# Window attention on one core: order and width of the score products on the tiles of TensorE

## The chip, the cores and the metric

The kernel runs on one core of a Trainium2 chip. The metric is the time of one execution on the device in microseconds. Before the change the median of three runs is 4113.76 us (4112.39 to 4114.41). A profile is one further execution, recorded instruction by instruction.

## The reference

The input x has 16 images of 56 x 56 positions with 384 channels, in fp32. Two layers follow each other.

```python
x = x + window_attention(group_norm(x, 32))
x = x + depthwise_3x3(group_norm(x, 32), sign(clip(w)))
```

The attention shifts the image by 3, cuts it into windows of 7 x 7 = 49 positions and works in each window with 12 heads of 32 channels:

```python
score = einsum('bhwqd,bhwkd->bhwqk', q, k) / sqrt(32) + rel[q, k]
# last row and last column of windows: -inf where q and k lie on different sides of the shift
attn = softmax(score)
out = einsum('bhwqk,bhwkd->bhwqd', attn, v) @ w_out.T + b_out
```

Everything is computed in fp32.

## The kernel before

An image is worked through in 8 strips of one row of windows (8 windows, 392 positions), each strip in two units of four windows. This gives 16 x 8 x 2 = 256 units. Channels lie on the 128 partitions in three blocks; a block holds four heads of 32 channels, so head i of a block lies on partitions 32i to 32i + 31.

For each strip TensorE makes queries and keys (`query_key`, L472, six blocks of 128 x 392), values (`value`, L485, three blocks) and the output projection (`project`, L655, three blocks), each with three accumulated matmuls. For each unit it makes the scores (`scores`, L526), the sums of the exponentials (`add_up`, L596) and the product with the values (`attend`, L616).

In a unit the four windows are two pairs: r is the pair, w the window of the pair. `scores` makes, for each block j, window w, pair r and head i, one product of 32 channels. Its weights (the stationary operand) are 64 columns of keys that begin with the 49 of the window, its moving operand the 49 queries. The result goes to partitions 64w to 64w + 63 of the PSUM bank i. A product thus uses 32 rows of the array, chosen by i, and 64 columns, chosen by w: one of eight tiles. With the loops in the order j, w, r, i, four products in a row go to four tiles, the next four (the other r) to the same four, and then w changes. The 15 rows behind the 49 keys receive products with keys of the next window, and nobody uses them.

`softmax` (L543, VectorE) reads all four banks, scales and adds a bias; `exponential` (L561, ScalarE) takes the exponential of all 128 rows in place and keeps a sum of each row, which after the last unit is only tested for being below 1e17. `add_up` writes into two of the four banks of the same scores tile (on all 128 partitions), where ScalarE (L634) and VectorE (L636) read it. The bias comes from `load_bias`, which fills a mask with zeros, loads its 2 x 49 valid rows from memory, and from `add_bias`. If the tests after the last unit fail, the program computes everything again with a softmax that subtracts the maximum (`fast` is False there, and keys and queries change places in `scores`).

The order of instructions is written out by hand (`manual_schedule`). `all_units` runs for each unit the heavy work in six steps, puts `scores` and `softmax` of the next unit behind the third or fourth of them, and fills in the light work (loading the next image, the convolution of the previous one) by due times. The steady order on TensorE over one strip is: sums and attention of the first unit, values and scores, queries and keys, sums and attention of the second unit, queries and keys, a third of the projection, scores, the rest of the projection, values. The convolution runs on VectorE (`tap`, L783), its input and the first image's come through the queues of POOL and SP. The scores tile has one buffer of four PSUM banks (`ps_s`); the other four banks go in turn to all other products (`ps`, `bank`).

Of the kernel before, what the change touches and what calls it, by code (L numbers as in the profile page):

```python
# [9 lines left out]
F32 = mybir.dt.float32  # L10
# [9 lines left out]
NEG = -1.0e30  # L20
# [14 lines left out]
def kernel(  # L35
# [12 lines left out]
    nc = tc.nc  # L48
    P = 128
    B, H, W, C = x.shape  # L50
    NH = rel_table.shape[1]
    D = C // NH
    NC = C // P
    HPC = P // D
    T = WIN * WIN
# [3 lines left out]
    UW = 4  # L59
    UPS = NW // UW  # L60
    NU = NS * UPS
    HT = 64
# [24 lines left out]
    small = ctx.enter_context(tc.tile_pool(name="small", bufs=2))  # L87
    ps_s = ctx.enter_context(tc.tile_pool(name="ps_s", bufs=1, space=bass.MemoryType.PSUM))
    ps = ctx.enter_context(tc.tile_pool(name="ps", bufs=4, space=bass.MemoryType.PSUM))

    def bank(name):
        return ps.tile([P, 512], F32, tag="mm", name=name)
# [18 lines left out]
    qk = const.tile([P, 2 * NC, ST + HT - T], F32, tag="qk", name="qk")  # L111
# [19 lines left out]
    def clear():  # L131
        for xl in xls:
            nc.gpsimd.memset(xl[:, NL - 1, :], 0.0)

        for t in spare:
            nc.gpsimd.memset(t[:, NL - 1, :], 0.0)

    def clear_more():
        nc.gpsimd.memset(power, -0.5)
        nc.gpsimd.memset(ones, 1.0)  # L140
        nc.gpsimd.memset(least, LEAST)
        nc.gpsimd.memset(seen, 0.0)
        for t in (qk[:, :, ST:], *hps, *accs):
            nc.gpsimd.memset(t, 0.0)
# [7 lines left out]
    def fetch_weights():  # L152

        rows = [w[r * P : (r + 1) * P, :] for w in (w_qkv, w_out) for r in range(w.shape[0] // P)]
        for n in range(0, len(rows), NC):
            wl = xpool.tile([P, NC, ST], F32, tag="x", name=f"wl_{n}")
            for k in range(NC):
                nc.scalar.dma_start(wl[:, k, :C], rows[n + k])
            staged.append(wl)

    def load_weights(n):

        for k in range(NC):
            pw = bank(f"pw_{n}_{k}")
            for c in range(NC):
                nc.tensor.transpose(pw[:, c * P : (c + 1) * P], staged[n][:, k, c * P : (c + 1) * P], ident)
            dst, r = (wq_t, NC * n + k) if n < NC else (wo_t, k)
            copy = nc.scalar.copy if k == 1 else nc.vector.tensor_copy
            copy(dst[:, :, r * P : (r + 1) * P], pw[:, : NC * P].rearrange("p (c q) -> p c q", c=NC))
# [20 lines left out]
    def load_bias(queue, first_q, last_q, fast):  # L190


        if not loaded_bias:
            rel = ypool.tile([P, NC, WIN, R], F32, tag="y", name="rel").rearrange("q c h w -> q (c h w)")[:, : T * NH]
            nc.gpsimd.memset(rel, 0.0)
            loaded_bias.append(rel)
        rel = loaded_bias[0]
        flat = rel.rearrange("q (a n) -> q a n", a=WIN)
        for q in range(first_q, last_q):
            qr, qc = divmod(q, WIN)  # L200
            first = qr * REL + qc if fast else (WIN - 1 - qr) * REL + (WIN - 1 - qc)
            row = rel_table[first : first + 1, :]
            src = bass.AP(
                tensor=row.tensor,
                offset=row.offset,
                ap=[[NH, 1], [REL * NH, WIN], [1, WIN * NH]],
            )
            queue.dma_start(flat[q : q + 1], src)
        if last_q < T:
            return  # L210
        queue.dma_start(flat[HT : HT + T], flat[0:T])
        mask = ypool.tile([P, NC, WIN, R], F32, tag="y", name="mask").rearrange("q c h w -> q (c h w)")[:, : 2 * T]
        mask = mask.rearrange("q (v k) -> q v k", v=2)
        nc.gpsimd.memset(mask, 0.0)
        for w in range(2):
            queue.dma_start(mask[w * HT : w * HT + T], wmask[0:T, :, 0:T])
        loaded_bias.append(mask)
# [151 lines left out]
    def fetch(s):  # L369
        b, r = divmod(s, NS)  # L370
        xl = staging(s)
        first = r * WIN + SHIFT
        for odd in range(2):
            t, end = 0, (WIN + 1 - odd) // 2
            while t < end:
                row = (first + odd + 2 * t) % H
                n = min(end - t, (H - row + 1) // 2)
                rows = x[b, row : row + 2 * n - 1 : 2].rearrange("t w c -> w t c")
                here = xl[odd * W : (odd + 1) * W, t : t + n, :]
                for lo, hi in ((SHIFT, SHIFT + 48), (SHIFT + 48, W), (W, R)):  # L380
                    nc.sync.dma_start(here[lo - SHIFT : hi - SHIFT], rows[lo % W : (hi - 1) % W + 1])
                t += n

    def load(s, c):
        b, r = divmod(s, NS)
        if (0, b) not in stats:
            stats[0, b] = small.tile([P, NC, NS, 6], F32, tag="st0", name=f"st0_{b}", bufs=1)
        if c == 0:
            xs[s] = xpool.tile([P, NC, ST], F32, tag="x", name=f"x_{s}")
        pt = bank(f"pl_{s}_{c}")  # L390
        for t in range(NL):

            n = min(LT, max(ST - t * LT, HT + 1))
            nc.tensor.transpose(
                pt[:, t * LT : t * LT + n], staging(s)[:n, t, c * P : (c + 1) * P], ident[:n, :n]
            )
        nc.scalar.copy(
            xs[s][:, c, :].rearrange("p (w r c) -> p r w c", r=WIN, c=WIN),
            pt[:, :ST].rearrange("p (r w c) -> p r w c", w=NW, c=WIN),
        )  # L400
        nc.vector.bn_stats(stats[0, b][:, c, r, :], xs[s][:, c, :])
# [111 lines left out]
    def scores(u, fast):  # L513


        s, n = divmod(u, UPS)
        pp = ps_s.tile([P, HPC, 512], F32, tag="s", name=f"ps_{u}")
        for j in range(NC):
            for w in range(2):
                for r in range(2):  # L520
                    for i in range(HPC):
                        part = slice(i * D, (i + 1) * D)
                        q0 = (n * UW + 2 * r + w) * T
                        row, col = (w, r) if fast else (r, w)
                        k0 = (2 * j + col) * T
                        nc.tensor.matmul(  # L526
                            pp[row * HT : (row + 1) * HT, i, k0 : k0 + T],
                            qk[part, NC * fast + j, q0 : q0 + HT],
                            qk[part, NC * (not fast) + j, q0 : q0 + T],
                            start=True,  # L530
                            stop=True,
                        )
        raw[u] = pp

    def softmax(u, fast):
# [482 lines left out]
    with tc.manual_schedule():  # L1018
        nc.scalar.preload_act_table_set("natural_log_exp_and_others")
        clear()  # L1020
        staged.append(None)
        for s in range(2 + len(spare)):
            fetch(s)
        staged.clear()
        fetch_weights()
        clear_more()
        load_bias(nc.gpsimd, 0, 38, True)
        for s in range(NS):
            for c in range(NC):
                load(s, c)  # L1030
            if s + 2 + len(spare) < NS:
                fetch(s + 2 + len(spare))
            if s % 2 and s > 1:
                load_weights(s // 2 - 1)
        norm_gather((0, 0), nc.sync)
        clear_again()
        for xl in xls:
            nc.gpsimd.memset(xl, 0.0)
        norm_scale((0, 0), nc.sync, nc.vector)
        load_bias(nc.gpsimd, 38, T, True)  # L1040
        load_weights(NC)
        load_depthwise()
        add_bias(True)
        normalize(0)
        all_units(True)


        worst = small.tile([P, 2], F32, tag="worst", name="worst")
        for n in range(2):
            nc.vector.tensor_scalar(reach[:, n], reach[:, n], MOST[n], None, ALU.is_lt)  # L1050
        nc.vector.tensor_reduce(worst[:, 0:1], reach.rearrange("p n u -> p (n u)"), AX.X, ALU.min)
        fine = small.tile([P, B + NC], F32, tag="fine", name="fine")
        nc.vector.tensor_scalar(fine, seen, 1.0e37, None, ALU.is_lt)
        nc.vector.tensor_reduce(worst[:, 1:2], fine, AX.X, ALU.min)
        pf = bank("pf")
        nc.tensor.matmul(pf[:, 0:2], ones, worst, start=True, stop=True)
        both = small.tile([P, 1], F32, tag="both_fine", name="both_fine")
        nc.vector.tensor_reduce(both, pf[:, 0:2], AX.X, ALU.add)
        nc.vector.tensor_scalar(again, both, -1.0, 2.0 * P, ALU.mult, ALU.add)
# [65 lines left out]
```

## Time and profile before

| | |
|---|---|
| median of the runs | 4113.76 us |
| profiled execution | 4109.91 us, span 4108.1 us |
| TensorE matmuls busy | 4017.7 us (98%) |
| TensorE weight loads busy | 2490.6 us |
| VectorE busy | 3496.3 us (85%) |
| ScalarE busy | 2236.7 us (54%) |
| GpSimd busy | 1873.2 us (46%) |
| scores, L526 | 24576 matmul passes and 24576 weight loads |

PE stands for matmuls, PEld for the weight loads, which overlap them; DVE is VectorE, ACT ScalarE, POOL GpSimd, SP the engine that only issues transfers. In a line of the groups, the part behind the names gives the size of the weights (rows * columns) and the shape of the moving operand, then the count, the busy time in us with the mean of one in ns, and the idle time of the engine ahead of them with what ended it. An fp32 product appears as two weight loads and two matmul passes. Busy time counts a moment once, however many passes overlap in it; the durations of single passes are modelled, their starts are not.

### The profile page before, as it was taken

What the parts mean: (1) busy time and instruction counts of PE and PEld (TensorE: products, weight loads), DVE (VectorE), ACT (ScalarE), POOL (GpSimd) and SP (SyncE); (2) the same over time, 40 slices, a digit from 0 to 9 for tenths busy, and PEclk for the clock granted to TensorE, in tenths of its full rate; (3) what the DMA queues carried; (4) which work ended last, traced back from release to release, by engine and by line L of the source; (5) the groups of instructions that cost most, each with busy time, mean ns of one, the idle gap of its engine ahead of it and who ended that gap; (6) DMA issues with size and microseconds to landing.
All of it is one profiled execution on the core that took longest, in us unless ns stands there. A gap on an engine that the chain in (4) does not pass through costs nothing.

```text
span 4108.1 us, 144986 instructions
## 1 busy us (share of the span) xinstructions
PE 4017.7 (98%) x63161; PEld 2490.6 (61%) x63161; DVE 3496.3 (85%) x3711; ACT 2236.7 (54%) x4654; POOL 1873.2 (46%) x3165
## 2 busy tenths in 40 slices
PE   5999999999999999999999999999999999999997
PEld 3666666666666666666666666666666666666656
DVE  4555989889898998989889898998989889898897
ACT  2545646555555655655555564655656555565552
POOL 5444535545453555545445452554545455452100
PEclk8999999999999999999999999999999999999998
DMA  4434556555655655556565655655556565554544
GB/s 94 78 61 89 111 101 126 106 107 103 118 114 110 117 110 108 111 98 127 107 114 104 112 115 105 117 117 100 114 101 122 105 123 109 102 123 77 108 101 110
DMA packets 1523990, 438.92 MB, mean 107 GB/s; under 512 B 1458970, under 2 KB 1473979, under 8 KB 1523346
## 3 DMA queue, kind: packets, MB, share of 16 engines
q1 hardware_dynamic: 1432680, 267.66, 38.1%
q0 software_dynamic: 87648, 159.12, 15.4%
q8 instruction: 499, 8.18, 0.8%
q10 hardware_dynamic: 3018, 2.78, 0.3%
q14 instruction: 145, 1.19, 0.1%
HBM read 169.63 MB, written 158.46 MB: 80 GB/s over the span
## 4 chain that ended last, share of the span: by engine, by line
PE 50%; issue 18%; POOL 13%; DVE 8%; DMA 7%; SPq 2%; ACT 1%; DVEq 0%; ACTq 0%; POOLq 0%
PE pq L472 21%; PE pv L485 10%; PE py L655 9%; POOL xl L419 8%; PE ps L526 4%; DVE o L783 4%; PE po L616 3%; DMA mvd<-mv 2%; PE ps L596 2%; POOL dev L268 2%; DMA xl<-in_x_dram 1%; DMA gt<-mvd 1%; SPq L508 1%; DMA mid<-y 1%; DVE e L543 1%
## 5 line engine op out<-in xcount | busy, mean ns | idle before, releaser
L472 PE MATMUL pq<-xn,wq_t 128*128 128x392 f32 x4608 | 1586.7, 497 | 0.1
L419 POOL DMA_DIRECT2D xl<-in_x_dram x1980 | 1332.9, 723 | 147.3 <-DVE xt L436 92.7
L783 DVE SCALAR_TENSOR_TENSOR o<-hp,dw_t,o 128x1568 f32<-128x1568 f32 x752 | 1378.8, 1834 | 5.4
L472 PEld LDWEIGHTS pq<-xn,wq_t 128*128 128x128 f32 x4608 | 846.2, 188 | 596.3 <-issue 1.5
L485 PE MATMUL pv<-xn,wq_t 128*128 128x392 f32 x2304 | 815.9, 497 | 8.1 <-DVE y L663 7.0
L655 PE MATMUL py<-ot,wo_t 128*128 128x392 f32 x2304 | 816.4, 499 | 3.0 <-DVE ot L644 3.0
L479 ACT COPY qk<-pq 128x392 f32<-128x392 f32 x768 | 369.4, 483 | 641.5 <-PE pq L472 640.3
L675 POOL COPY y<-y 128x63 f32<-128x63 f32 x128 | 53.3, 416 | 1320.8 <-DVE y L663 1320.8
L485 PEld LDWEIGHTS pv<-xn,wq_t 128*128 128x128 f32 x2304 | 424.2, 188 | 308.2 <-DVE y L663 8.7
L655 PEld LDWEIGHTS py<-ot,wo_t 128*128 128x128 f32 x2304 | 426.4, 190 | 300.1 <-DVE ot L644 10.5
L561 ACT ACTIVATE e<-e 128x1176 f32<-128x1176 f32 x256 | 303.2, 1184 | 439.0 <-DVE e L543 437.9
L636 DVE SCALAR_TENSOR_TENSOR ln<-ps,inv 128x588 f32<-128x588 f32 x256 | 196.1, 766 | 368.5 <-ACT inv L635 367.9
L492 ACT COPY vt<-pv 128x392 f32<-128x392 f32 x384 | 189.2, 493 | 411.9 <-PE pv L485 411.8
L526 PEld LDWEIGHTS ps<-qk 32*64 32x64 f32 x24576 | 307.2, 131 | 144.5 <-issue 108.3
L616 PEld LDWEIGHTS po<-e,v 49*32 49x32 f32 x24576 | 352.2, 105 | 55.5 <-issue 11.4
L543 DVE SCALAR_TENSOR_TENSOR e<-ps,bias 128x1176 f32<-128x1176 f32 x256 | 347.4, 1357 | 12.6 <-PE ps L526 12.2
L616 PE MATMUL po<-e,v 49*32 49x49 f32 x24576 | 345.5, 212 | 10.3 <-DMA v<-vq 9.6
L526 PE MATMUL ps<-qk 32*64 32x49 f32 x24576 | 339.3, 226 | 2.0 <-DVE ln L636 2.0
L448 ACT COPY x<-xt 128x196 f32<-128x196 f32 x720 | 225.6, 368 | 178.3 <-DVE xt L436 178.1
L496 DVE STREAM_TRANSPOSE vq<-vt 128x512 f32<-128x512 f32 x384 | 266.0, 694 | 9.9 <-ACT vt L492 6.5
L663 DVE TENSOR_TENSOR y<-py,x 128x392 f32<-128x392 f32 x384 | 213.6, 556 | 48.2 <-PE py L655 44.7
L461 ACT ACTIVATE xn<-x,coef 128x392 f32<-128x392 f32 x384 | 247.1, 711 | 13.2 <-DMA coef<-cod 13.2
(173 smaller groups left out, 3287.4 us busy)
## 6 DMA issues: line engine op xcount, KB each, us to landing
v<-vq SPq DMA_DIRECT2D x2048, 48.0 KB
xb<-mid SPq DMA_DIRECT2D x90, 855.5 KB
out_dram<-o SPq DMA_DIRECT2D x736, 98.0 KB
mid<-y POOLq DMA_DIRECT2D x112, 619.5 KB
xl<-in_x_dram POOLq DMA_DIRECT2D x1260, 52.5 KB
mid<-y POOLq DMA_DIRECT2D x15, 354.0 KB
xl<-in_x_dram POOLq DMA_DIRECT2D x180, 28.0 KB
mid<-y POOLq DMA_DIRECT2D x15, 265.5 KB
```

The source lines that it names most:

```text
L419: nc.gpsimd.dma_start(xz[i * D + lo : i * D + hi, c, k : k + n, :], flat[token : token + n * (hi - lo)].rearrange("(k t) c -> t k c", k=n) ...
L461: nc.scalar.activation(xn[:, c, :, :T], xs[s][:, c, :].rearrange("p (w t) -> p w t", t=T), AF.Identity, bias=coef[:, c, 1:2], scale=coef[: ...
L472: nc.tensor.matmul(pq[:, :ST].rearrange("p (w t) -> p w t", t=T), wq_t[:, c, m * P : (m + 1) * P], xn[:, c, :, :T], start=(c == 0), stop=( ...
L479: nc.scalar.copy(qk[:, m, :ST], pq[:, :ST])
L485: nc.tensor.matmul(pv[:, :ST].rearrange("p (w t) -> p w t", t=T), wq_t[:, c, 2 * C + m * P : 2 * C + (m + 1) * P], xn[:, c, :, :T], start= ...
L496: nc.vector.transpose(vq[:, :, :, m].rearrange("p h n d -> p n h d"), vt[:, m].rearrange("p (n w) (j b) -> p n (w j) b", w=2, b=D),)
L526: nc.tensor.matmul(pp[row * HT : (row + 1) * HT, i, k0 : k0 + T], qk[part, NC * fast + j, q0 : q0 + HT], qk[part, NC * (not fast) + j, q0 ...
L543: nc.vector.scalar_tensor_tensor(e, pp[:, :, : NC * 2 * T].rearrange("q i (n k) -> q i n k", k=T), QSCALE, bias[:, int(s % NS == NS - 1)]. ...
L561: nc.scalar.activation(flat, flat, AF.Exp, accum_out=reach[:, 0, u : u + 1])
L616: nc.tensor.matmul(po[w][i * D : (i + 1) * D, (2 * j + r) * T : (2 * j + r + 1) * T], vs[s][keys, n * 2 + r, h * D : (h + 1) * D], by_head ...
L655: nc.tensor.matmul(py[:, :ST], wo_t[:, c, m * P : (m + 1) * P], ots[s][:, c, :], start=(c == 0), stop=(c == NC - 1),)
L783: nc.vector.scalar_tensor_tensor(acc, by_half(hp[:, dy : dy + BR, dx : dx + W]), dw_t[:, c, t : t + 1], acc, ALU.mult, ALU.add)
```

## The change

In `scores` the loops over w, r and i become a loop over r and one over eight values k, which takes the heads 0 to 3 twice and alternates w: head i with w = 0, 1, 0, 1 in the first four and w = 1, 0, 1, 0 in the second four. Eight products in a row go to eight tiles. The weights are the 49 keys alone, and the output is 49 rows. The rows between the windows are therefore no longer written by `scores`: they hold zeros from a clearing at the start, or sums that `add_up` wrote there. For them the mask is filled with -1e30 where it was 0, so that their exponentials are zero. The scores tile is made once, ahead of the loops, in place of once per unit. In the second computation (`fast` False) the weights keep 64 columns and the mask keeps zeros.

```diff
+    score_banks = ps_s.tile([P, HPC, 512], F32, tag="s", name="score_banks")
...
-        nc.gpsimd.memset(mask, 0.0)
+        nc.gpsimd.memset(mask, NEG if fast else 0.0)
...
-        pp = ps_s.tile([P, HPC, 512], F32, tag="s", name=f"ps_{u}")
+        pp = score_banks
+        rows = T if fast else HT
         for j in range(NC):
-            for w in range(2):
-                for r in range(2):
-                    for i in range(HPC):
-                        part = slice(i * D, (i + 1) * D)
-                        q0 = (n * UW + 2 * r + w) * T
-                        row, col = (w, r) if fast else (r, w)
-                        k0 = (2 * j + col) * T
-                        nc.tensor.matmul(
-                            pp[row * HT : (row + 1) * HT, i, k0 : k0 + T],
-                            qk[part, NC * fast + j, q0 : q0 + HT],
-                            qk[part, NC * (not fast) + j, q0 : q0 + T],
-                            start=True,
-                            stop=True,
-                        )
+            for r in range(2):
+                for k in range(2 * HPC):
+                    i, w = k % HPC, (k + k // HPC) % 2
+                    part = slice(i * D, (i + 1) * D)
+                    q0 = (n * UW + 2 * r + w) * T
+                    row, col = (w, r) if fast else (r, w)
+                    k0 = (2 * j + col) * T
+                    nc.tensor.matmul(
+                        pp[row * HT : row * HT + rows, i, k0 : k0 + T],
+                        qk[part, NC * fast + j, q0 : q0 + rows],
+                        qk[part, NC * (not fast) + j, q0 : q0 + T],
+                        start=True,
+                        stop=True,
+                    )
...
         clear()
+        nc.vector.memset(score_banks, 0.0)
```

## The prediction

> **What bounds the kernel now.** I read the engines' shares of the span first, then the busy times of the steady middle.
>
> ```profile
> PE 4017.7 (98%) x63161; PEld 2490.6 (61%) x63161; DVE 3496.3 (85%) x3711; ACT 2236.7 (54%) x4654; POOL 1873.2 (46%) x3165
> 2000.00:3000.00 1000.00, 997.25 (x15955) 610.56 (x15951) 888.87 (x928) 568.70 (x1188) 500.31 (x836) 1.00 0.58 111
> ```
>
> In the second line the numbers after the length are PE, PEld, DVE, ACT and POOL. TensorE is never out of work: 997 of 1000 us, at full clock. DVE is next with 889. So the time is the sum of TensorE's batches, and a microsecond taken out of one comes off the span, until DVE is reached. Next the groups of instructions for the scores (L526), the attention product (L616) and the operation that reads the scores.
>
> ```profile
> L526 PEld LDWEIGHTS ps<-qk 32*64 32x64 f32 x24576 | 307.2, 131 | 144.5 <-issue 108.3
> L543 DVE SCALAR_TENSOR_TENSOR e<-ps,bias 128x1176 f32<-128x1176 f32 x256 | 347.4, 1357 | 12.6 <-PE ps L526 12.2
> L616 PE MATMUL po<-e,v 49*32 49x49 f32 x24576 | 345.5, 212 | 10.3 <-DMA v<-vq 9.6
> L526 PE MATMUL ps<-qk 32*64 32x49 f32 x24576 | 339.3, 226 | 2.0 <-DVE ln L636 2.0
> ```
>
> 24576 = 256 batches x 96: each of the 48 fp32 products of a batch is two weight loads and two matmul passes. A busy PE isn't a fast PE, since these overlap: the price of a batch is the distance from its first start to the start of the next batch. The timeline of PE over one strip gives it.
>
> ```profile
> 2030.37 1.14 PE L616 MATMUL po<-e,v 49*32 49x49 f32 x96
> 2031.45 4.22 PE L485 MATMUL pv<-xn,wq_t 128*128 128x392 f32 x12
> 2035.59 1.32 PE L526 MATMUL ps<-qk 32*64 32x49 f32 x96
> 2036.84 8.17 PE L472 MATMUL pq<-xn,wq_t 128*128 128x392 f32 x24
> ```
>
> Scores: 2036.84 - 2035.59 = 1.25 us. Attention, with as many passes of as many columns and eight tiles in rotation (two row groups by four column groups): 2031.45 - 2030.37 = 1.08 us. Read start by start from the trace, the scores take 1.246 us almost every time (127 of 127 where query_key follows, within 0.1 us; 96 of 127 within 0.02 us where project follows). The attention's best is 1.072 us, met on both of its places.
>
> Where do the scores lose? Busy times by stretch, of L526 alone, all from one beginning, so that each count tells how many passes (first count) and loads (second) have begun:
>
> ```profile
> 2005.20:2005.38 0.18, 0.10 (x9) 0.10 (x12) 1.00 0.00 0
> 2005.20:2005.58 0.38, 0.30 (x33) 0.30 (x34) 1.00 0.00 0
> 2005.20:2005.78 0.58, 0.50 (x43) 0.50 (x45) 1.00 0.00 0
> 2005.20:2005.98 0.78, 0.70 (x62) 0.70 (x66) 1.00 0.07 2
> 2005.20:2006.18 0.98, 0.90 (x83) 0.90 (x85) 1.00 0.10 3
> 2005.20:2006.38 1.18, 1.10 (x96) 1.10 (x96) 1.00 0.09 3
> ```
>
> and the same for an attention batch:
>
> ```profile
> 2030.30:2030.57 0.27, 0.20 (x19) 0.27 (x16) 1.00 0.48 66
> 2030.30:2030.77 0.47, 0.40 (x36) 0.47 (x36) 1.00 0.32 44
> 2030.30:2030.97 0.67, 0.60 (x60) 0.67 (x60) 1.00 0.23 31
> 2030.30:2031.17 0.87, 0.80 (x82) 0.87 (x81) 1.00 0.17 24
> ```
>
> Three parts in a scores batch. (1) By 2005.58, 0.30 us in, 34 loads (17 products) have begun: these were queued already. (2) A hole: the 35th load starts 0.344 us in. (3) The other 31 products take until about 1.10 us, 10 passes per 0.1 us (43 to 83 in 0.40 us), where the attention does 12 (36 to 60 in 0.20 us), that is 16.7 ns a product. Single starts show why. Loads of four neighbours are 16.7 ns apart (344, 361, 378, 394 ns), then a load for a tile used four products ago waits: 394 to 461, and 117 ns lie between two first loads of one tile. Where the loop changes w, the next four go to other tiles and there is no wait (511, 528, 544, 561 ns). So the loop's two values of r, which hit the same four tiles one after the other, cost about 50 ns once per eight products.
>
> **The Trainium skill.** "TensorEngine Tiling (Array Packing)", Key Properties, says different tiles run loads and matmuls in parallel, and 32x64 has eight. The trace agrees where w changes. "TensorE: Matmul & The Clock Gate", Part 3, says a load overlaps matmuls in flight only when the row group differs. Here the trace differs: the loads at 528 to 561 ns go to row groups whose matmuls on the other column tile had just begun (515 to 565 ns). The same page, LDWEIGHTS, prices a load at columns / 1.2 ns: 53 ns for 64, 41 for 49; the trace has 55 ns from a tile's first load to its second (344 to 399), and no 49-column load. "Runtime: NRT & Kernel Launch", Instruction fetch mechanics, says instructions come in 16 KiB blocks of 256, mostly hidden. The page shows 499 packets and 8.18 MB on the instruction queue, 16.4 KB each; whether it is hidden matters below.
>
> **The change part by part.**
> Order and width. Products on one tile are now eight apart: 8 x 16.7 = 133 ns, against the 117 ns a tile needs now and an estimated 117 - 2 x 12 = 93 with 49 columns. The wait goes. What is next is the issue of instructions, 16.7 ns a product. A batch then is: start of the 18th product 0.344 us (unchanged), 30 further products x 16.7 = 0.501, one load and one pass until the last pass begins, 41 + 41 ns = 0.08 (my estimate, 49 columns or rows at 1.2 per ns), and 0.145 us from the last pass to the next batch as now. Sum 1.07 us, against 1.246; the attention's clean 1.072 says the same. The hole is uncertain: if the queue refills because something finishes, the first product ends earlier (its load is shorter by 12 ns); if because the queue runs empty, eight tiles empty it at the 6.6 ns a pass with which the attention opens, 34 x 6.6 = 0.22, + 0.057 for the gap seen now = 0.28 us, another 0.06 less. Between both I take 1.056, a gain of 0.19 us; ends 0.174 and 0.25.
>
> Issue stalls. Now a late instruction is caught by the backlog: sequencer 16.7 ns a product, array 24.4 ((1.10 - 0.344) / 31). With the array waiting for the sequencer it isn't. The attention shows the price: of its 127 batches ahead of query_key the mean is 1.185 us, 0.113 over the best, with holes of 60 to 110 ns at changing places. Per product, 0.113 / 39 (nine are queued at its start), so 31 products could lose 0.09 us. Against that, the scores ahead of query_key show not one late batch now, those ahead of project 31 of 127. I take half, 0.045; ends 0 and 0.09.
>
> Net 0.19 - 0.045 = 0.145 us x 256 = 37 us. Ends: (0.174 - 0.09) x 256 = 22 and 0.25 x 256 = 64.
>
> One tile for all units in place of one per unit: in the built order of TensorE's instructions the waits stand where they stood: at the first product on DVE in half of the batches, at the 1st, 17th and 33rd on ACT in the others. Nothing. The clearing of the tile: one DVE operation, 2048 elements a row; by L543 (1176 in 1.357 us) an estimated 2.4 us, while DVE does nothing until 17.33 us. Uncovered it would cost those 2.4. The mask's fill has another value and the same size. DVE's and ACT's operations keep their shapes; the rows between windows hold old sums or zeros plus the mask, so their exponentials are zero. No DMA is added or moved. The matmuls behind the scores start earlier; in the steady middle DVE goes from 0.889 to 0.898 of the time (30.6 us a strip less 0.29), so it stays behind.
>
> Against the profiled execution, 4109.91 us (span 4108.1), this gives 4073; the median of the runs shown is 3.9 above it, and I take that as base: 4113.8 - 37 = 4077.
>
> **Rivals.**
> (A) As above, stalls partly seen: 25 to 50 us, 4064 to 4089.
> (B) The refill comes earlier and stalls stay hidden: 50 to 70 us, 4044 to 4064. For it: the hole starts just after the last queued load (287 ns). Against: the attention stalls.
> (C) Stalls in full, or DVE's taps (1.8 us each) make TensorE wait for banks more often (now 7.0 us at L485): 8 to 25 us, 4089 to 4105.
> (D) The change doesn't do what it says: something else than the tile sets 24.4 ns a product, for instance a limit per row group of 93 ns for four: 31 / 4 x 93 = 0.72 against 0.756 us, 0.04 us, or nothing: 4104 to 4114. Against: the eight loads in one run.
> (E) Slower: taking turns between two column tiles of one row group makes each load wait for the pass in flight there, as the skill's sentence would have it, with both passes of both products in line: 4 x 41 = 164 ns for four products, 41 each; 31 x (41 - 24.4) = 0.51 us, 132 us: 4245. It decides from 24.4 ns a product on. Against: the same eight loads; for: the trace shows such a turn only once per eight products, and no load of 49 columns.
>
> **How the numbers follow.** A 0.60, B 0.13, C 0.14, D 0.06, E and other ways to lose 0.07. A measurement of this kernel can tell about 0.2%, 8.2 us. Faster: A, B, C and a bit of D, 0.88; same 0.05; slower 0.07. The range takes in A and most of B and C: 4055 to 4100.
>
> **What would show it.** Scores batches of about 1.06 us with a tail of later ones up to 1.2; loads of 49 columns, and eight loads 16.7 ns apart in one run; still 12 passes per 0.1 us after the hole. TensorE as busy as before and DVE near 0.90. Wrong, if passes stay at 10 per 0.1 us (D), fall below it (E), or if batches after the scores grow longer (C).

## The result and the profile after

The changed kernel takes 4081.35 us (median of 4 runs, 4078.99 to 4082.26) beside 4113.34 us before; the ratio is 0.9925, with a 95% interval of 0.9912 to 0.9937. That is 32 us less, where 37 were forecast. A later series of the same kernel gave 4083.65 beside 4113.10 us (ratio 0.9929, 0.9915 to 0.9942), 29 us less. The profiled execution has a span of 4079.4 us, 28.7 below that of before.

First the engines' shares and the steady middle of the kernel after, in the order PE, PEld, DVE, ACT, POOL:

```profile
PE 3981.1 (98%) x63161; PEld 2447.1 (60%) x63161; DVE 3495.8 (86%) x3712; ACT 2231.7 (55%) x4654; POOL 1870.2 (46%) x3165
2000.00:3000.00 1000.00, 994.95 (x16087) 604.45 (x16087) 896.86 (x937) 566.29 (x1189) 495.10 (x835) 1.00 0.60 113
```

DVE went from 889 to 897 us in the 1000. TensorE is still nearly always busy, but its idle time in this stretch grew from 2.75 to 5.05 us. The groups (lines have moved: L529 was L526, L619 was L616, L546 was L543):

```profile
L619 PE MATMUL po<-e,v 49*32 49x49 f32 x24576 | 347.1, 212 | 13.4 <-DMA v<-vq 11.9 <-issue 0.2
L546 DVE SCALAR_TENSOR_TENSOR e<-score_banks,bias 128x1176 f32<-128x1176 f32 x256 | 347.2, 1356 | 10.7 <-PE score_banks L529 10.7
L529 PE MATMUL score_banks<-qk 32*49 32x49 f32 x24576 | 298.2, 218 | 2.6 <-DVE ln L639 2.2 <-issue 0.2
L529 PEld LDWEIGHTS score_banks<-qk 32*49 32x49 f32 x24576 | 265.7, 118 | 145.4 <-issue 108.9 <-DVE ln L640 12.8 <-DVE vq L498 8.9
```

The scores' union of busy time falls from 339.3 to 298.2 us, the shape is 32*49, and VectorE's operation on them is unchanged. In the timeline of PE a scores batch and its neighbours:

```profile
2016.73 4.22 PE L487 MATMUL pv<-xn,wq_t 128*128 128x392 f32 x12
2020.88 1.14 PE L529 MATMUL score_banks<-qk 32*49 32x49 f32 x96
2021.95 8.17 PE L474 MATMUL pq<-xn,wq_t 128*128 128x392 f32 x24
```

2021.95 - 2020.88 = 1.07 us from start to start, where it was 1.25. The same batch by stretches from one beginning, with the count of passes and then of loads that have begun:

```profile
2020.80:2020.98 0.18, 0.10 (x11) 0.10 (x19) 1.00 0.60 128
2020.80:2021.18 0.38, 0.30 (x33) 0.30 (x34) 1.00 0.58 112
2020.80:2021.38 0.58, 0.50 (x51) 0.50 (x54) 1.00 0.43 87
2020.80:2021.58 0.78, 0.70 (x72) 0.70 (x74) 1.00 0.32 64
2020.80:2021.78 0.98, 0.90 (x93) 0.90 (x96) 1.00 0.47 83
```

The opening looks alike (33 passes, 34 loads after 0.30 us), but afterwards 18, 21 and 21 passes begin in each 0.20 us, where it was 10, 19 and 21, and the last ones are under way 0.17 us earlier.

From all starts in the two traces, summed over the strips:

| batch, start to next start | before, us | after, us | difference |
|---|---|---|---|
| scores, 256 | 327.7 | 287.1 | -40.6 |
| sums and attention, first units, 127 | 258.6 | 266.5 | +7.9 |
| sums and attention, second units, 127 | 216.5 | 215.0 | -1.5 |
| queries and keys ahead of project, 127 | 515.8 | 519.8 | +4.0 |
| first third of project, 127 | 263.6 | 264.6 | +1.0 |
| all else | | | +0.5 |
| span | 4108.1 | 4079.4 | -28.7 |

So the edit itself brought 40.6 us, more than forecast, and 12 us were lost again in batches that it doesn't touch. A trace is one execution: in that of the later series (span 4083.8 us) the scores gain 40.4 us and the span 24.3, so that 16 us are lost again. The gain of the scores repeats, the loss varies.

### The profile page after: what moved, and what is told of

Same layout as the page of the kernel before. It is cut to its first block, busy times and chain, and to the rows that moved or that the text cites. A ratio compares the mean times of both kernels' runs of the same rounds, so it can differ in the third digit from the quotient of the medians.

```text
span 4079.4 us, 144987 instructions
## 1 busy us (share of the span) xinstructions
PE 3981.1 (98%) x63161; PEld 2447.1 (60%) x63161; DVE 3495.8 (86%) x3712; ACT 2231.7 (55%) x4654; POOL 1870.2 (46%) x3165
## 4 chain that ended last, share of the span: by engine, by line
PE 46%; issue 16%; POOL 12%; DVE 12%; DMA 7%; SPq 4%; ACT 2%; DVEq 0%; ACTq 0%; POOLq 0%
PE pq L474 19%; PE pv L487 10%; PE py L658 8%; POOL xl L421 8%; DVE o L786 5%; PE score_banks L529 3%; PE po L619 3%; SPq L510 3%; DMA xl<-in_x_dram 2%; PE score_banks L599 2%; DMA mvd<-mv 2%; DVE e L546 1%; POOL dev L270 1%; DMA gt<-mvd 1%; DVE xt L438 1%
## 5 line engine op out<-in xcount | busy, mean ns | idle before, releaser
L639 DVE SCALAR_TENSOR_TENSOR ln<-score_banks,inv 128x588 f32<-128x588 f32 x256 | 195.9, 765 | 349.2 <-ACT inv L638 349.2
L619 PEld LDWEIGHTS po<-e,v 49*32 49x32 f32 x24576 | 352.2, 105 | 60.4 <-issue 14.3
L619 PE MATMUL po<-e,v 49*32 49x49 f32 x24576 | 347.1, 212 | 13.4 <-DMA v<-vq 11.9
L546 DVE SCALAR_TENSOR_TENSOR e<-score_banks,bias 128x1176 f32<-128x1176 f32 x256 | 347.2, 1356 | 10.7 <-PE score_banks L529 10.7
L529 PEld LDWEIGHTS score_banks<-qk 32*49 32x49 f32 x24576 | 265.7, 118 | 145.4 <-issue 108.9
L529 PE MATMUL score_banks<-qk 32*49 32x49 f32 x24576 | 298.2, 218 | 2.6 <-DVE ln L639 2.2
L666 DVE TENSOR_TENSOR y<-py,x 128x392 f32<-128x392 f32 x384 | 213.3, 555 | 43.1 <-PE py L658 39.2
```

The lines of the kernel that those rows point to most:

```text
L529: nc.tensor.matmul(pp[row * HT : row * HT + rows, i, k0 : k0 + T], qk[part, NC * fast + j, q0 : q0 + rows], qk[part, NC * (not fast) + j, ...
L546: nc.vector.scalar_tensor_tensor(e, pp[:, :, : NC * 2 * T].rearrange("q i (n k) -> q i n k", k=T), QSCALE, bias[:, int(s % NS == NS - 1)]. ...
L619: nc.tensor.matmul(po[w][i * D : (i + 1) * D, (2 * j + r) * T : (2 * j + r + 1) * T], vs[s][keys, n * 2 + r, h * D : (h + 1) * D], by_head ...
```

## The experiments

### The two halves of the edit

The order alone, with weights of 64 columns, against the changed kernel:

```diff
-        rows = T if fast else HT
+        rows = HT
...
-        nc.gpsimd.memset(mask, NEG if fast else 0.0)
+        nc.gpsimd.memset(mask, 0.0)
```

> The new order with weights of 64 columns as before (the mask zero again). Tile theory: the distance of eight products, 133 ns at 16.7 ns a product, is above the 117 ns that a tile needs for two loads of 64 columns and two passes, so the wait per eight products goes with the order alone. Against the changed kernel only the opening and the end are longer, by two and by one loads that are 12 ns longer each: a scores batch of 1.11 us in place of 1.073 (before: 1.246), and about 4090 us in all. Rival, the width did it: batches of 1.2 us or more, 4103 us or more.

The width alone, in the order of before, against the changed kernel:

```diff
-            for r in range(2):
-                for k in range(2 * HPC):
-                    i, w = k % HPC, (k + k // HPC) % 2
+            for k in range(4 * HPC):
+                    i, r, w = k % HPC, k // HPC % 2, k // (2 * HPC)
```

> Weights of 49 columns in the old order. Tile theory: a tile needs 117 - 24 = 93 ns, its next product comes after four, 67 ns, so a wait of 26 ns in place of 50 stays, once per eight products; with a shorter opening (25 ns) a batch of about 1.12 us, 8 passes per 0.1 us lost less often, 4092 us. Rival, the order did it all: 1.22 us or more and 4105 us or more.

| kernel | scores batch, median us | time, us (ratio to before, interval) |
|---|---|---|
| before | 1.246 | 4113.02 |
| order alone | 1.148 | 4098.00 (0.9964, 0.9949 to 0.9978) |
| width alone | 1.121 | 4091.66 (0.9949, 0.9933 to 0.9966) |
| both (the change) | 1.073 | 4081.35 (0.9925, 0.9912 to 0.9937) |

The width alone did what was expected of it (1.12 us, 4092 us). The order alone fell short: 1.148 in place of 1.11 us. With the width alone a tile's first loads are 92 ns apart (median starts at 319 and 411 ns), where 93 were worked out; before the change it was 117. Neither half did it all, so both rivals of these runs are out. One thing these runs can't separate: the eight tiles have eight outputs, a half of one PSUM bank each, so that a product which returns to a tile also returns to its half bank. That the tile is what is waited for is argued: the wait shrank by 25 ns when two loads per product became 12 ns shorter each. The groups of the two kernels show the same; first the order alone, then the width alone (its L528 is the same product):

```profile
L529 PE MATMUL score_banks<-qk 32*64 32x49 f32 x24576 | 317.0, 228 | 2.6 <-DVE ln L639 2.0 <-issue 0.6
```

```profile
L528 PE MATMUL score_banks<-qk 32*49 32x49 f32 x24576 | 309.3, 213 | 3.1 <-DVE ln L638 2.2 <-issue 0.8
```

Why the order fell short is in its stretches:

```profile
2000.00:2000.36 0.36, 0.30 (x33) 0.30 (x34) 1.00 0.00 0
2000.00:2000.56 0.56, 0.50 (x46) 0.50 (x50) 1.00 0.00 0
2000.00:2000.76 0.76, 0.70 (x68) 0.70 (x69) 1.00 0.07 2
2000.00:2000.96 0.96, 0.90 (x87) 0.90 (x91) 1.00 0.10 3
```

Between 2000.56 and 2000.76 it keeps the attention's pace (22 passes in 0.20 us), so the wait per eight products is gone. But it has two holes: the load of the 18th product starts 0.345 us into the batch (median of all batches), and in a batch followed start by start the flow of first loads, 16.7 ns apart, breaks off again and resumes at 0.690 us, twice that. The changed kernel has the same pair at 0.319 and 0.638 us, the second only 36 ns wide. Before the change the first was at 0.344 us.

### What a batch is bound by now

The changed kernel with 25 keys and 25 queries of each product, the other scores left out (the softmax takes the bias alone, so that the values stay finite):

```diff
-        rows = T if fast else HT
+        rows, cols = (25, 25) if fast else (HT, T)
...
-                        pp[row * HT : row * HT + rows, i, k0 : k0 + T],
+                        pp[row * HT : row * HT + rows, i, k0 : k0 + cols],
...
-                        qk[part, NC * (not fast) + j, q0 : q0 + T],
+                        qk[part, NC * (not fast) + j, q0 : q0 + cols],
...
-            QSCALE,
+            0.0 if fast else QSCALE,
```

> The changed kernel with 25 of the 49 keys as weights and 25 of the 49 queries as moving columns; the other scores are left out and the softmax takes the bias alone (the scores times zero), with operations of the same shapes. Issue theory: 16.7 ns a product after the hole stay, as it is the issue of instructions that sets them; only the opening ends earlier, by the 20 ns of a shorter load and the 20 ns of a shorter pass, and the end by as much: a batch of about 0.99 us, some 20 us less than the changed kernel, 4060 us. Rival, tiles or array still set the pace: 31 products in half the time, batches of 0.75 us, 4000 us. On the hole: if it ends when the first passes finish it moves from 0.32 to 0.28 us; if it is a fixed latency of the queue it stays at 0.32.

And with 25 keys and all 49 queries, `(25, T)`:

> The changed kernel with 25 of the 49 keys as weights, all 49 queries moving; the other scores are left out and the softmax takes the bias alone. On the hole that ends with the 18th product: it ended after 0.345 us with 64 columns, 0.319 with 49 and 0.260 with 25 keys and 25 queries. Two loads and one pass plus a constant of 196 ns fit all three (columns and rows over 1.2 per ns) and give 0.279 here; one load and two passes would give 0.299. A second hole, as long after the first as the first after the start, should be gone, since 17 products take 0.283 us; a batch of about 0.95 us.

The first took 4058.17 us (ratio 0.9861, 0.9845 to 0.9878) with batches of 0.915 us; the second 4073.66 us (one run) with batches of 1.003 us. Both batches missed what was expected (0.99 and 0.95 us), in part by the second hole, which the first of them no longer had and the second still had. That the time of the first came out near the expected 4060 us is luck: against the changed kernel a batch fell by twice the forecast 0.08 us, and the runs by little more than the forecast 20 us. Half-size products do not halve a batch, so neither tiles nor array set its pace. The stretches of the first, a batch that starts at 2003.18:

```profile
2003.10:2003.28 0.18, 0.10 (x22) 0.10 (x29) 1.00 1.40 131
2003.10:2003.48 0.38, 0.30 (x37) 0.30 (x39) 1.00 1.71 130
2003.10:2003.68 0.58, 0.50 (x61) 0.50 (x63) 1.00 1.52 119
2003.10:2003.88 0.78, 0.70 (x85) 0.70 (x87) 1.00 1.49 113
```

24 passes in each 0.20 us: 16.7 ns a product, the pace at which the attention ran, without a second hole. In the opening 29 loads have begun after 0.10 us, then hardly any until 0.26 us: with smaller products the first 17 are begun sooner, and the hole ahead of the 18th stays.

The hole's end, by the size of a product (columns of weights x moving columns), as the median start of the 35th load:

| 64 x 49 | 49 x 49 | 25 x 49 | 25 x 25 |
|---|---|---|---|
| 0.345 us | 0.319 us | 0.295 us | 0.260 us |

It moves with the length of a load and of a pass. My formula of two loads and one pass gave 0.279 for the third, one load and two passes 0.299; 0.295 is nearer to the second, but that formula doesn't fit the step from 64 to 49 columns. So what it is made up of stays open. The second hole obeys a simpler rule: in the batches followed start by start it ends at 0.690, 0.638 and 0.590 us, twice the first. That fits a queue which takes 17 products (34 loads and 34 passes), and in which a place is free again only one such time later. Seventeen products at 16.7 ns take 0.283 us; where the time is longer, a hole of the difference opens (0.319 - 0.283 = 36 ns, as seen; 0.295 - 0.283 = 12, as seen), and where it is shorter, as with 0.260, there is none. The expected disappearance of the hole at 25 x 49 was therefore wrong by these 12 ns. The reading as a queue of places is argued from these numbers, not shown by itself.

### Where 12 us came back

TensorE's waits of the changed kernel (engine, line waited for: total us, times, longest):

```profile
PE po L619 <- DMA v<-vq: 11.9, 15, 5.4
PE pv L487 <- DVE y L666: 8.6, 13, 0.7
PE py L658 <- DVE ot L647: 3.8, 5, 3.0
```

Before the change they were (that for the values is 9.6 us, in the line of L616 in the prediction):

```profile
PE pv L485 <- DVE y L663: 7.0, 13, 0.6
PE py L655 <- DVE ot L644: 3.0, 1, 3.0
```

All three have grown, though by less than 5 us together; the rest of the 12 us are passes that start late while earlier ones still run. And all three hang on VectorE: it transposes the values that the transfers then move, drains project's banks and divides `ot`. To test it, both kernels ran with four of the eight taps of the convolution left out for the first 15 images:

```diff
             for i, t in enumerate((0, 1, 2, 3, 5, 6, 7, 8)):
-                at(when + step * i / 9, tap, p, k, c, t)
+                if i % 2:
+                    at(when + step * i / 9, tap, p, k, c, t)
```

> The kernel before with four of the eight outer taps of the convolution left out for the first 15 images (360 VectorE operations of 1.83 us less, 0.66 ms of VectorE). It is the base of the next run. TensorE has the same work, so only its waits for VectorE go: 4095 to 4112 us.

> The changed kernel with the same taps left out. The scores batches got 40.6 us shorter in the profile and the span only 28.7: 8 us came back in the attention batches of the first units, 4 us between queries and project. Theory, they come back as VectorE is too late for the shorter schedule: then the difference to the kernel before with the same taps left out is 40 us. Rival, they come back by waits and issue holes that VectorE has no part in (transfers of the values): the difference stays 32 us or less.

The pair took 4107.98 and 4070.17 us (ratios to the kernel before 0.9987, 0.9980 to 0.9993, and 0.9896, 0.9880 to 0.9911): 37.8 us apart, and 39.8 in the spans (4110.2 and 4070.4). The scores' batches of this pair differ by 39.2 us, sums and attention of the first units are equal (248.3 and 248.4 us), and so is the stretch ahead of project (515.1 in both). The groups with fewer taps no longer name VectorE ahead of `pv`, first the kernel before, then the changed one:

```profile
L485 PE MATMUL pv<-xn,wq_t 128*128 128x392 f32 x2304 | 815.9, 498 | 1.2 <-ACT xn L461 1.2
L616 PE MATMUL po<-e,v 49*32 49x49 f32 x24576 | 344.9, 212 | 8.4 <-DMA v<-vq 7.8 <-issue 0.2
```

```profile
L487 PE MATMUL pv<-xn,wq_t 128*128 128x392 f32 x2304 | 815.8, 497 | 1.2 <-ACT xn L463 1.2
L619 PE MATMUL po<-e,v 49*32 49x49 f32 x24576 | 344.7, 212 | 8.1 <-DMA v<-vq 7.8
```

So in these traces the stretches that VectorE feeds take nothing back once it has less to do: with the convolution at full size, parts of the freed time turn into waits for what VectorE delivers. The runs say it less sharply: 37.8 us apart beside 32.0 and 29.5 in the two series with all taps, with some 7 and 5 us of uncertainty either way (worked out from the intervals of the ratios). And the pair has losses of its own: the scores batches ahead of query_key are 13.5 and 14.8 us longer in all than with all taps, in both kernels alike.

### The late instructions

After the change 45 of the 127 scores batches ahead of project are 23 to 184 ns late, but only 5 of the 127 ahead of query_key. The former have two waits on ScalarE more, at the 17th and 33rd product. The blocks backwards take these waits away:

```diff
-        for j in range(NC):
+        for j in reversed(range(NC)):
             for r in range(2):
```

> The changed kernel with the blocks j of the scores in the order 2, 1, 0. The first product then waits for ScalarE's last copy, and the two waits at the 17th and 33rd product of the batches ahead of project go. If these waits let late instructions through (45 of those 127 batches are late by 20 to 160 ns, only 5 of the 127 ahead of query_key, which have no such waits), the late ones go and the kernel gets 4 to 5 us faster, 4077 us. Rival, instruction fetch or other traffic: as many late batches, 4081 us.

It took 4085.35 us (ratio 0.9931, 0.9917 to 0.9945), and 39 of the 127 are late. The waits are not the cause of most of them. With half the taps 50 of the 127 were late, so VectorE's load isn't either. Nor do fetches of instructions explain most: in the trace of the changed kernel the queue that fetches instructions in packets of 16 KB had none in flight during 36 of the 45 late batches. The cause stays open.

### Three tries for more

The first units' attention has holes at its first eight products, each of which waits for two transfers of the values. Three kernels tried to get these waits out of the way. The attention ahead of the sums:

```diff
-                    if fast:
-                        add_up(u)
...
-                    attend(u, fast)
+                    po = attend(u, fast)
+                    if fast:
+                        add_up(u)
+                        invert(u)
+                    take(u, po)
```

`take` holds the two evacuations that stood at the end of `attend`.

> The changed kernel with the attention product ahead of the sums on TensorE (the evacuation stays behind the sums' logarithm). Of the attention batches of a strip's first unit the median is 1.41 us against a clean 1.074, with holes of 42 and 83 ns at the first seven products, each of which waits for two transfers of the values. Theory: these waits are handled one by one by the sequencer, 125 ns for each product, and cost time only because eight short sums ahead don't keep the array busy; behind value's long passes they are hidden. Then 127 batches get 0.3 us shorter: 38 us, about 4045 us. Rival: the values themselves are late, or the later sums make project wait for ot: no gain, 4075 us or more.

It took 4140.90 us (ratio 1.0065, 1.0048 to 1.0082), slower than before the change. The idle time of the weight loads ahead of project (L662 here), by what ended it:

```profile
  PE pq L474: 96.3, 125
  DVE ot L651: 18.2, 17
```

The stretch from queries and keys to project grew from 519.8 to 559.4 us: in the median strip project's passes start 0.09 us after the end of the matmuls ahead of it, where in the changed kernel they start 0.16 us before it. The profile names these matmuls (`pq`) in 125 strips, as they ended last, but project's first load starts 115 to 117 ns after the end of the division (L651) in each of the 128 strips, also where the matmuls had ended 0.8 us before. So it waits for `ot`, and the rival holds: the sums, about 0.9 us later, are the start of the chain logarithm, reciprocal, division, and project stands at its end. First units' sums and attention had a median of 1.853 us in place of 1.929, and a mean of 2.186 in place of 2.098.

A small product that takes the waits ahead of value's long passes:

```diff
         pv = bank(f"pv_{s}_{m}")
+        if m == 0 and s - 1 in vs:
+            nc.tensor.matmul(pv[:65, 0:HPC], ones[:, :65], vs[s - 1][:, 0, 0:P:D], start=True, stop=True)
```

> The changed kernel with one small product more per strip, ahead of value's first: 65 columns of ones times four columns of the values of the strip before, into a bank that value then overwrites. It takes the sixteen waits for the transfers of the values away from the first eight attention products of a strip's first unit and puts them behind the long passes of project. Theory: the sequencer handles them one at a time, which costs the first units' batches 0.33 us (median 1.41 against 1.074 us), and there the array is busy meanwhile. Then sums and attention of the first unit get down to the second unit's median, 1.72 us in place of 1.93, or below; 127 x 0.2 to 0.33 = 27 to 42 us, less 127 x 0.1 us for the product: 4052 to 4067 us. Rival, the values are late themselves, and the wait only moves to an earlier place: 4080 us or more.

4190.17 us (ratio 1.0184, 1.0170 to 1.0198). TensorE's waits:

```profile
PE pv L487 <- DMA v<-vq: 93.4, 38, 14.1
```

Theory and rival both had a part. Sums and attention of the first units fell to 1.593 us in the median, 208.9 us in all, 58 us less than in the changed kernel. But in 38 strips the values are not there yet at the earlier place, and 93 us are spent on that alone. These waits cost a second time. The granted clock, 1.00 from 102 to 3965 us in the changed kernel, is 0.50 here in 22 stretches between 105 and 3950 us, 85 us together; at half the clock that is up to 43 us more (an estimate). The same at the head of the sums, with two products of 32 columns:

```diff
         su = raw[u][:, 0:2, : NC * 2 * T]
+        if u % UPS == 0:
+            for w in range(2):
+                keys = slice(w * HT, w * HT + T)
+                nc.tensor.matmul(su[:D, w, 0:HPC], ones[keys, :D], vs[u // UPS][keys, 0, 0:P:D], start=True, stop=True)
```

> The changed kernel with the touch of the values moved to the head of the sums: two products of 32 columns of ones times four columns of the values, in the sums' tiles and into columns that the sums then overwrite. The place before value's first product made the first units' sums and attention 1.593 us (median 1.93 before), 58 us in all, but stood 2.7 us earlier, so that values that the attention just met were waited for (93 us at that place). Here the sequencer takes the sixteen waits while value's passes run, and a late transfer is waited for only about 0.5 us earlier than in the changed kernel. Theory: 127 x 0.3 us less some 10 us of lateness and 4 us for the products: 4050 to 4062 us. Rival, the late values set the time of the first units and the sixteen waits were hidden behind them: 4075 us or more.

4095.44 us (ratio 0.9963, 0.9951 to 0.9975), 14 us slower than the changed kernel. The median of the first units' sums and attention fell to 1.656 us, but the upper quarter rose from 2.06 to 2.17 us and the highest tenth from 2.72 to 3.03 us, so that the sum is 264.0 us where it was 266.5: the waits for the values grew from 11.9 to 31.0 us. Another 12 us were added between value and scores, and here too by the clock: nine stretches of 3.4 us at half the clock between 105 and 3950 us, each begun within 4 us of a pause of TensorE of 1.4 to 2.6 us, and the passes of values that fall into them take 5.0 to 5.8 us where they take 4.15 else. One of them, in the timeline and in the stretches (the 0.50 is the granted clock):

```profile
2446.25 0.16 PE L599 MATMUL score_banks<-v,ones 49*32 49x4 f32 x1 [1.76 <-DMA v<-vq]
2447.74:2451.15 3.41, 3.41 (x26) 1.91 (x12) 2.31 (x4) 3.09 (x6) 0.42 (x2) 0.50 0.54 189
```

The changed kernel's pauses in the same part of its trace are 0.75 us at most, and it has no such stretch. So time freed ahead of the values becomes a wait for them, and a wait that is long enough slows what follows.

> The changed kernel again, beside the run before it on the same chip: 4081 us, within 4 us.

The changed kernel beside the first of these tries: 4083.65 us, as told above. No kernel of the study was faster than it with all of the work.

## Why the prediction was right

The bound. TensorE's batches did set the time, and the saving went through to the span, but not in full. "It stays behind", said of VectorE from 0.889 to 0.898 of the time, is the step that didn't hold: the average was right (0.897), but 12 of the 40.6 us were lost again in the trace, as far as the runs with fewer taps show by late deliveries of VectorE. The prediction had this as part of rival C, as more waits at `pv`; that grew by 1.6 us only, and most came back at the first units' attention and ahead of project.

The wait per eight products. Shown: with order and width together it is gone, and with the width alone a shorter one stays, as large as computed (1.12 us). That products on alternate column tiles of one row group run side by side is shown too: a row group takes a product every 67 ns (4 x 16.7), while the two passes of one product alone are an estimated 82 ns (a pass of 392 columns takes 328 ns, so one of 49 takes 41). Rival E, which took the sentence of the Trainium skill ("TensorE: Matmul & The Clock Gate", Part 3) on loads and row groups at its word, is out, and so is D.

The batch. Forecast 1.056 us, measured 1.073. Two terms were off, in opposite directions: the hole ended 25 ns earlier where 14 were taken off (1.070 to 1.056), and a second hole of 36 ns was not foreseen, since the pace of 16.7 ns was carried on through all 31 products. The end of the batch was 8 ns shorter. In the kernel with the order alone the same omission is larger (62 ns), which is why its expectation was short.

The late instructions. Forecast 0.045 us a batch, measured 0.022 (0.007 ahead of query_key and 0.037 ahead of project, as means over 1.073). The asymmetry that the traces showed beforehand stayed; its cause is open.

The sum. 0.145 us a batch was forecast and 0.159 came (40.6 / 256), 37 us and 40.6 us. With 12 us lost again the profile shows 28.7 us, the runs 32. That 37 lies so near to 32 is in part luck: a clean batch gained 0.17 us where 0.19 were forecast, the late instructions cost half of what was taken, and the 12 us stand in no term of the sum. The clearing of the tile (1.76 us, 2.4 estimated) and the mask's fill cost nothing that could be seen in the time, and the waits stood where they had stood.

## What to carry to other kernels

Price a burst of small products by the distance from its first start to the next batch's, not by busy time, and look for what repeats: products that return to a tile too soon cost a wait, and loads of columns that nobody uses make that wait longer. Once tiles are no longer the limit, what limits is a pace that the size of the products doesn't change (here read as the pace of issue, which is argued), and smaller products then bring little (half the keys and queries took only 0.16 of 1.07 us off a batch). An engine at nine tenths of the time is no bound on average, but what it delivers late can take back a part of a saving elsewhere: here 30 to 40% in two profiles. And look at the granted clock behind each longer pause of TensorE before a slower kernel is put down to the pause alone.

## What the runs showed of the hardware

Behind the first hole an fp32 product on one of eight tiles began every 16.7 ns at best, two loads and two passes each, whatever its size (25 x 25 or 49 x 49). The first products of a batch go faster, a pass every 6.7 ns at its start, but only 17 of them; then there was a hole until 0.26 to 0.345 us after the first start, by the size of the products, and, where that was above 0.283 us, a second one that ended at twice that time. Products on two column tiles of one row group, 67 ns apart, did not hinder each other. Sixteen waits for transfers at eight products cost about 0.27 to 0.34 us of TensorE where only short work stood ahead of them (median 1.929 us against 1.656 and 1.593 with the waits moved). And pauses of TensorE of 1.4 to 2.6 us were followed by 3.4 us at half the granted clock in nine places of one trace.
